# Last context attention of a four-layer network on one core: squares from SBUF, one fixed order for three engines, and the first keys turned beside the layer ahead

## The chip, the cores and the metric

The kernel runs on one core of one Trainium2 chip. The metric is the device time of one execution in microseconds (us), as the median of several runs. A profile of one execution of the kernel before is at hand: its own time, what each engine did and when, and what each instruction waited for. Engines are named as the profile does: PE is TensorE (matmuls), PEld its weight loads, DVE is VectorE, ACT is ScalarE, POOL is GpSimd, SP issues most DMAs.

## The reference, cut to what matters

The network has four layers, each of a cross attention on a context of 2 x 2048 tokens, a mixing block and a feed-forward block, on 2 x 128 tokens of width 256. The change touches the end of the third layer and the cross attention of the fourth, which is this:

```python
def _L3_xattn_ref(draft_hidden, context_hidden, Wq, Wk, Wv, Wo, q_norm_w, k_norm_w, context_position_ids, draft_position_ids):
    B, CTX, DRAFT, D = (2, 512, 64, 256)
    H, KVH, HD = (16, 4, 128)
...
    q = (draft_hidden @ Wq.T).reshape(bsz, draft_len, H, HD)
    q = _rms_norm(q, q_norm_w).transpose(0, 2, 1, 3)
    kv_in = jnp.concatenate([context_hidden, draft_hidden], axis=1)
    k = (kv_in @ Wk.T).reshape(bsz, total_len, KVH, HD)
    v = (kv_in @ Wv.T).reshape(bsz, total_len, KVH, HD).transpose(0, 2, 1, 3)
    k = _rms_norm(k, k_norm_w).transpose(0, 2, 1, 3)
...
    q = _rope(q, draft_position_ids)
    k = _rope(k, full_position_ids)
...
    probs = jax.nn.softmax(scores, axis=-1)
    attn = jnp.einsum('bhqk,bhkd->bhqd', probs, v)
    return attn @ Wo.T
```

Keys and queries are normalised by the root of their mean square (`_rms_norm`), turned by position (`_rope`), and 16 heads of queries share 4 heads of keys and values. With the 128 own tokens, each of the two sequences has 2176 keys, 17 tiles of 128. The block ahead of it is a linear layer with a low-rank update whose two of eight experts are chosen by a gate.

## The kernel before, in words

**Groups.** `l3_xattn` works through eight groups (4 key heads x 2 sequences). For a group, `projected` (line 1448) makes the keys of 8 context tiles in one PSUM tile called `wide` (1024 columns, two of them exist), VectorE copies it to `kq` in SBUF and ScalarE writes its squares to `rot`, reading the same PSUM tile. `own` (1459) does the same for the 128 own tokens: keys, values, and four heads of queries. `summed` (1474) sums the squares on VectorE and takes the root on ScalarE; `rotated` (1479) scales by the inverse root, by the norm's weights, and rotates, all on VectorE, into `rot`. `turn` (1505) transposes 21 tiles of `rot` on TensorE into `kT` and `qT`; VectorE and ScalarE take turns at copying them out of the two PSUM tiles `tr`. `scores` (1521) is called once for each of four heads: four matmuls of 512 keys into two `wide` tiles and one of 128 into `one`; VectorE evicts each with its maximum, makes the scaled maximum `nb`, and ScalarE writes the exponential with its sum. `attend` (1539) transposes the probabilities tile by tile (17 times four), ScalarE copies them to `pT`, and a matmul with `v` adds up in `py`. `out` multiplies by the output weights and adds to `x`.

**What lies beside what.** While group `now` is scored and attended, group `nxt` is projected, normalised and rotated: its first 8 tiles after the first head's scores, its first sums and own tokens after the second head's, its last 8 tiles and the other sums after the fourth head's, its rotations ahead of `attend`. The first group is prepared beside the causal attention of layer three, in smaller steps (line 1583 on).

**What sets the order.** The framework's scheduler puts instructions into each engine's queue by readiness and by program order. The class `InOrder` wraps an engine so that each instruction is queued behind whatever the program put on that engine ahead of it. In `l3_xattn` TensorE and VectorE are wrapped from line 1601 on; ScalarE is not, so there the scheduler chooses.

**The seam.** `l2` and `l3_xattn` are generators; `next(last)` in `l2` runs the next piece of `l3_xattn`. The last call to `linear` (line 1313) is the linear layer for the second sequence. It has three steps: projections, the gate's small operations, and the sum. Beside it `g.busy` (line 137) puts 8 and 12 filler matmuls on TensorE. `l3_xattn` hands it a PSUM bank at line 1602 and goes on with line 1603 only when `linear` has ended: values loaded, 21 tiles turned, then the first scores.

Of the kernel before, what the change touches and what calls it, by code (L numbers as in the profile page):

```python
# [12 lines left out]
F32 = mybir.dt.float32  # L13
# [4 lines left out]
AF = mybir.ActivationFunctionType  # L18
# [4 lines left out]
P = 128  # L23
B = 2
D = 256
# [1093 lines left out]
def l2(g, ctxT, codes, last):  # L1119
# [9 lines left out]
    with tc.tile_pool(name="l2", bufs=1, side="right", reuse_waits="tile") as p:  # L1129
        def mine(name, shape, src):  # L1130
            t = p.tile(list(shape), F32, name=name)
            nc.sync.dma_start(t, src)
            return t

        wkv, wq, wg = (g.load("L2_xattn_" + k) for k in ("Wkv", "Wq", "Wg"))
        bg = mine("bg", [P, 2], g.ins["L2_xattn_bg"])
        wxo = mine("wxo", [P, 2, D], g.ins["L2_xattn_Wo"])
        wqk, wv, wo = (g.load("L2_attn_" + k) for k in ("Wqk", "Wv", "Wo"))
        bqk = mine("bqk", [P, 512], g.ins["L2_attn_bqk"].partition_broadcast(P))
        bv = mine("bv", [P, D], g.ins["L2_attn_bv"].partition_broadcast(P))  # L1140
        bo = mine("bo", [P, D], g.ins["L2_attn_bo"].partition_broadcast(P))
        rot = mine("rot2", [P, 2, 8], g.ins["rope16"])
        cos = rot[:, 0, :].unsqueeze(1).to_broadcast([P, 2 * H, 8])
# [98 lines left out]
        def causal_attention(b):  # L1242
# [5 lines left out]
            g.project(ps, lambda c: xnT[:, c, :], lambda c: wqk[:, c, :])  # L1248
            qk = p.tile([P, 2 * H, 16], F32, tag="qk", name="qk")
            nc.vector.tensor_tensor(qk.rearrange("p h d -> p (h d)"), ps, bqk, ALU.add)  # L1250
            pv = g.mm([P, D])
            g.project(pv, lambda c: xnT[:, c, :], lambda c: wv[:, c, :])
            pad = p.tile([P, 2 * H, 32], F32, tag="pad", name="pad")
            nc.gpsimd.memset(pad, 0.0)
            t1 = p.tile([P, 2 * H, 8], F32, tag="t1", name="t1")
            t2 = p.tile([P, 2 * H, 8], F32, tag="t2", name="t2")
            x1, x2 = qk[:, :, 0:8], qk[:, :, 8:16]
            nc.vector.tensor_tensor(t1, x1, cos, ALU.mult)
            nc.gpsimd.tensor_tensor(t2, x2, sin, ALU.mult)
            t3 = p.tile([P, 2 * H, 8], F32, tag="t3", name="t3")  # L1260
            t4 = p.tile([P, 2 * H, 8], F32, tag="t4", name="t4")
            nc.vector.tensor_tensor(t3, x2, cos, ALU.mult)
# [3 lines left out]

            v = p.tile([P, H, 17], F32, tag="v", name="v")
            nc.gpsimd.memset(v[:, :, 16:17], 1.0)
            nc.vector.tensor_tensor(v[:, :, 0:16], pv.rearrange("p (h d) -> p h d", d=16), bv.rearrange("p (h d) -> p h d", d=16), ALU.add)
            yield  # L1270
            qkT = p.tile([P, 8, P], F32, tag="qkT", name="qkT")
            for j in range(2):
# [7 lines left out]
            for j in range(4):  # L1280

                sc = g.mm([P, 4, P])
                r0 = 32 * j
                for i in range(4):
                    nc.tensor.matmul(sc[:, i, :], lhsT=qkT[r0:r0 + 16, i, :], rhs=qkT[r0:r0 + 16, 4 + i, :], start=True, stop=True)
                S = p.tile([P, 4, P], F32, tag="S", name="S", bufs=4)
                nc.vector.scalar_tensor_tensor(S, sc, -0.25, g.causal.unsqueeze(1).to_broadcast([P, 4, P]), ALU.mult, ALU.subtract)
                nm = g.sm([P, 4], "nm4", bufs=4)
                nc.vector.tensor_reduce(nm, S, AX.X, ALU.min)
                for i in range(4):  # L1290
                    nc.scalar.activation(S[:, i, :], S[:, i, :], AF.Exp, bias=nm[:, i:i + 1], scale=-1.0)
                if b == 0 or j == 0:
                    g.values.step(1)
                tp = g.tr([P, 4, P])
                for i in range(4):
                    nc.tensor.transpose(tp[:, i, :], S[:, i, :], g.ident)
                pT = p.tile([P, 4, P], F32, tag="pT", name="pT", bufs=3)
                nc.vector.tensor_copy(pT, tp)
                for i in range(4):
                    h = 4 * i + j  # L1300
                    nc.tensor.matmul(av[:, h, :], lhsT=pT[:, i, :], rhs=v[:, h, :], start=True, stop=True)
                yield
# [10 lines left out]
        def linear(b, bank):  # L1313
# [5 lines left out]
            pl, pa, po = ps[:, 0:E], ps[:, P:2 * P], ps[:, D:2 * D]  # L1319
            if b == 1:  # L1320
                g.busy(8, ps[:, 0:2 * P])
            g.project(pl, lambda c: xT[:, c, :], lambda c: gw[:, c, :])
# [31 lines left out]
            nc.vector.tensor_tensor(ga, ga, pg, ALU.mult)  # L1354
            if b == 1:
                g.busy(12, po)
            for c in range(2):
# [25 lines left out]
        for _ in causal_attention(1):  # L1383
            next(third, None)
            next(last)
        bank = None
        third = linear(1, lambda: bank())
# [4 lines left out]
        for _ in third:  # L1392
            pass

# [4 lines left out]
def l3_xattn(g, ctxT, cos, sin, values):  # L1399
# [10 lines left out]
    SCALE = float(np.float32(1.0 / np.sqrt(HD)))  # L1410
    pe, dve, pp = nc.tensor, nc.vector, None
    with ExitStack() as ctx:
# [18 lines left out]
        class Group:  # L1431
# [16 lines left out]
            def projected(self, t, n=8):  # L1448
# [7 lines left out]
                dve.tensor_copy(self.kq[:, t:t + n, :], ks)  # L1456
                nc.scalar.activation(self.rot[:, t:t + n, :], ks, AF.Square)

            def own(self):
# [8 lines left out]
                dve.tensor_copy(self.kq[:, NT, :], kv[:, 0:HD])  # L1468
                nc.scalar.activation(self.rot[:, NT, :], kv[:, 0:HD], AF.Square)
                nc.scalar.copy(self.v[:, NT, :], kv[:, HD:2 * HD])  # L1470
                dve.tensor_copy(self.kq[:, KT:NR, :], pq)
                nc.scalar.activation(self.rot[:, KT:NR, :], pq, AF.Square)  # L1472

            def summed(self, lo, hi):
                rs = self.rs[:, lo:hi]
                dve.tensor_reduce(rs, self.rot[:, lo:hi, :], AX.X, ALU.add)
                nc.scalar.activation(rs, rs, AF.Sqrt, bias=g.eps6, scale=1.0 / HD)

# [26 lines left out]
            def turn(self):  # L1505

                self.kT = p2.tile([P, KT * P], F32, tag="kT", name="kT", bufs=1)
                self.qT = p2.tile([P, REP, P], F32, tag="qT", name="qT", bufs=1)
                for k, t in enumerate([KT] + list(range(0, KT, 4))):
                    n = min(4, KT - t) if t < KT else REP  # L1510
# [4 lines left out]
                    if k % 2:  # L1515
                        dve.tensor_copy(out, tp[:, 0:n, :])
                    else:
                        nc.scalar.copy(out, tp[:, 0:n, :])
                    yield

            def scores(self, r):

                S = p2.tile([P, KT, P], F32, tag="S", name="S", bufs=4)
                self.Ss.append(S)
# [11 lines left out]
                dve.tensor_scalar(nm, nm, -SCALE, None, ALU.mult)  # L1536
                nc.scalar.activation(Sf, Sf, AF.Exp, bias=nm, scale=SCALE, accum_out=self.rz[:, r:r + 1])  # L1537

            def attend(self):

                py = pp.tile([P, REP, P], F32, tag="py", name="py", bufs=1)

                def turned(t):
                    tp = g.tr([P, REP, P])
                    for r in range(REP):
                        pe.transpose(tp[:, r, :], self.Ss[r][:, t, :], g.ident)
                    pT = p2.tile([P, REP, P], F32, tag="pT", name="pT", bufs=3)
                    nc.scalar.copy(pT, tp)  # L1548
                    return pT

                pT = turned(0)
                for t in range(KT):
                    nxt = turned(t + 1) if t + 1 < KT else None
                    pe.matmul(py, lhsT=self.v[:, t, :], rhs=pT, start=(t == 0), stop=(t == KT - 1))
                    pT = nxt
                self.yT = p2.tile([P, REP, P], F32, tag="yT", name="yT", bufs=1)
                nc.scalar.copy(self.yT, py)

# [23 lines left out]
        for t in range(0, NT, 2):  # L1582
            now.projected(t, 2)
            values.step()
            if t == 8:
                normed(0)
                now.own()
                now.summed(NT, NR)
            if t == 6:
# [10 lines left out]
        g.ps = pp = ctx.enter_context(tc.tile_pool(name="l3ps", bufs=1, space=PSUM, reuse_waits="tile"))  # L1600
        pe, dve = InOrder(tc, nc.tensor), InOrder(tc, nc.vector)
        yield lambda: pp.tile([P, 512], F32, tag="py", name="py", bufs=1)
        p2 = ctx.enter_context(tc.tile_pool(name="l3s", bufs=2, reuse_waits="tile"))
        now.load()
        for _ in now.turn():
            pass
        normed(1)
        for n in range(len(todo)):
            nxt = Group(*todo[n + 1]) if n + 1 < len(todo) else None
            if nxt:  # L1610
                nxt.load()
            now.Ss = []
            now.rz = g.sm([P, REP], "rz")
            for r in range(REP):
                now.scores(r)
                if nxt and r == 0:
                    nxt.projected(0)
                if nxt and r == 1:
                    nxt.summed(0, 8)
                    nxt.own()  # L1620
                if nxt and r == 3:
                    nxt.projected(8)
                    nxt.summed(8, NR)
            if nxt:
                nxt.rotated(0, 8)
                nxt.rotated(8, NR)
            now.attend()
            turn, out = nxt.turn() if nxt else iter(()), now.out()
# [667 lines left out]
```

## Time and profile before

| | us |
|---|---|
| median of 3 runs (1565.37 to 1567.48) | 1566.69 |
| the profiled execution | 1566.19 |
| its span in the profile | 1564.5 |
| TensorE busy | 1421.2 (91%) |
| VectorE busy | 1136.9 (73%) |
| ScalarE busy | 825.1 (53%) |
| mean granted TensorE clock | 0.913 of full speed |
| first score matmul of the last context attention | at 709.06 |
| start of the eighth group's scores | at 1113.90 |
| last output matmuls of the attention | until 1160.6 |

The page gives busy times over the whole span. A stage is read better from the chain of work that ended last (each step with what released it), from the timeline of a window, and from busy times in stretches, where the granted clock of TensorE stands third from the right as a share of full speed. In lines with a releaser, the idle time just ahead of an instruction is followed by "<-" and the instruction that ended it.

### The profile page before, as it was taken

The numbers are of one execution on the slowest core, as the hardware profiler recorded it, in microseconds if no ns is written. First come the engines' busy times: TensorE is split into PE (matmuls) and PEld (weight loads), VectorE is DVE, ScalarE is ACT, GpSimd is POOL, SyncE is SP. The second block draws the span as 40 slices with busy tenths as digits, with TensorE's granted clock in tenths as the row PEclk, the third lists the DMA queues.
The fourth block names the chain that finished last, engine by engine and source line by source line (L and its number), as shares of the span: only waits on it lengthen the run. The fifth ranks groups of instructions, "written<-read, shape, count | busy, mean of one in ns | idle before, by whom it ended". The sixth has DMA issues, their size and how long they took to land.

```text
span 1564.5 us, 18429 instructions
## 1 busy us (share of the span) xinstructions
PE 1421.2 (91%) x6932; PEld 879.7 (56%) x6932; DVE 1136.9 (73%) x1962; ACT 825.1 (53%) x1260; POOL 148.0 (9%) x140
## 2 busy tenths in 40 slices
PE   8759997898889999978998998998988999999988
PEld 5413333676556777655555555565544566666567
DVE  6889997576456476675775775775726999999976
ACT  3567775323334422435455455455437777777721
POOL 6620002020000000000000000000000111111110
PEclk9955555899999999979999999999989999999999
DMA  6799999644350341410001000000133222221110
GB/s 185 143 178 203 204 202 188 221 149 143 96 182 21 106 135 41 125 54 14 28 5 49 28 17 24 27 28 1 35 121 148 94 95 95 95 94 41 34 34 8
DMA packets 225427, 144.40 MB, mean 92 GB/s; under 512 B 177928, under 2 KB 203801, under 8 KB 220985
## 3 DMA queue, kind: packets, MB, share of 16 engines
q1 hardware_dynamic: 222128, 141.27, 34.5%
q10 hardware_dynamic: 3144, 1.76, 0.4%
q8 instruction: 55, 0.90, 0.2%
q0 software_dynamic: 64, 0.18, 0.1%
q14 instruction: 36, 0.29, 0.1%
HBM read 90.85 MB, written 8.65 MB: 64 GB/s over the span
## 4 chain that ended last, share of the span: by engine, by line
PE 65%; DVE 18%; ACT 9%; DMA 4%; issue 2%; POOL 2%; SPq 0%; DVEq 0%; ACTq 0%; POOLq 0%
PE mm L227 13%; PE mm L184 10%; PE wide L227 9%; PE py L227 7%; DVE S L227 6%; PE pb L227 6%; PE tr L227 5%; DMA pT<-Si 2%; PE acc L1201 2%; PE sc L227 2%; PE acc L227 2%; ACT S L1537 1%; PE one L227 1%; DVE ro L227 1%; POOL kn L227 1%
## 5 line engine op out<-in xcount | busy, mean ns | idle before, releaser
L227 DVE TENSOR_SCALAR_CACHE_REDUCE S<-sc 128x1024 f32<-128x1024 f32 x128 | 150.6, 1219 | 6.8 <-PE sc L227 3.3
L227 PE MATMUL wide<-kT,qT 128*128 128x512 f32 x256 | 128.2, 637 | 25.2 <-ACT rot L1472 20.4
L227 PE MATMUL sc<-kT,qT 48*128 48x512 bf16 x256 | 130.4, 616 | 19.3 <-DMA kT<-kpad 6.5
L227 ACT ACTIVATE Si<-S,nb,sq 128x4096 int16<-128x4096 f32 (+1 forms) x35 | 122.7, 3506 | 43.0 <-issue 27.9
L227 PE MATMUL py<-pT,v 128*128 128x512 f32 x272 | 141.5, 606 | 3.3 <-ACT pT L1548 3.3
L1548 ACT COPY pT<-tr 128x512 f32<-128x512 f32 x136 | 78.2, 584 | 81.0 <-PE tr L227 81.0
L1537 ACT ACTIVATE S<-S,nb 128x2176 f32<-128x2176 f32 x32 | 67.5, 2109 | 93.5 <-DVE nb L227 93.5
L227 DVE TENSOR_SCALAR_CACHE_REDUCE S<-wide 128x1024 f32<-128x1024 f32 x64 | 78.3, 1224 | 51.8 <-PE wide L227 50.6
L227 PE MATMUL pb<-wb,xT 128*128 128x512 f32 x256 | 112.6, 592 | 0.0
L227 PEld LDWEIGHTS tr<-ident,S 128*128 128x128 f32 x544 | 67.8, 142 | 69.7 <-issue 38.8
L227 PEld LDWEIGHTS wide<-kT,qT 128*128 128x128 f32 x256 | 48.5, 203 | 82.7 <-issue 43.5
L227 PEld LDWEIGHTS <-pT 128*128 128x128 bf16 x1024 | 36.5, 105 | 94.8 <-issue 87.8
L227 PE MATMUL tr<-ident,S 128*128 128x128 f32 x544 | 83.1, 275 | 3.7 <-ACT S L1537 3.3
L227 PEld LDWEIGHTS pb<-wb,xT 128*128 128x128 f32 x256 | 48.9, 191 | 60.0 <-issue 55.6
L227 ACT ACT_TABLE_LOAD x53 | 68.0, 1283 | 3.7 <-PE mm L227 3.0
L227 ACT ACTIVATE bc<-pb,rs 128x128 f32<-128x128 f32 x256 | 68.0, 432 | 0.9 <-DVE rs L227 0.9
L227 ACT ACTIVATE bc<-pb 128x1024 f32<-128x1024 f32 x32 | 32.8, 1024 | 64.5 <-PE pb L227 64.5
L227 PE MATMUL mm<-m,xb 128*64 128x128 f32 x512 | 61.7, 279 | 2.9 <-DVE m L227 1.9
L184 PE MATMUL mm<-wvs,ctxT 128*128 128x512 f32 x128 | 61.3, 599 | 0.0
L227 PEld LDWEIGHTS mm<-m,xb 128*64 128x64 f32 x512 | 56.7, 139 | 6.7 <-DVE m L227 2.6
L227 DVE COPY kq<-wide 128x1024 f32<-128x1024 f32 (+2 forms) x28 | 24.0, 855 | 47.7 <-PE wide L227 27.6
L227 PE MATMUL mm<-xT,w 128*128 128x256 f32 x216 | 53.6, 395 | 0.0
(542 smaller groups left out, 2942.7 us busy)
## 6 DMA issues: line engine op xcount, KB each, us to landing
w<-in_L_ffn_w_dram SPq DMA_DIRECT2D x25, 384.0 KB
vs<-st SPq DMA_DIRECT2D x32, 256.0 KB
v<-vs SPq DMA_DIRECT2D x8, 1024.0 KB
wb<-in_L_attn_WB_dram SPq DMA_DIRECT2D x8, 1024.0 KB
wb<-in_L_attn_WC_dram SPq DMA_DIRECT2D x8, 1024.0 KB
bb<-in_L_attn_BC_bias_dram SPq DMA_DIRECT2D x8, 1024.0 KB
ctxT<-in_ctxT_dram SPq DMA_DIRECT2D x15, 512.0 KB
w<-in_ctx_dram SPq DMA_DIRECT2D x8, 512.0 KB
```

Source lines behind the costliest of these rows:

```text
L184: self.nc.tensor.matmul(out, lhsT=lhsT(c), rhs=w(c), start=(c == 0), stop=(c == n - 1))
L227: return lambda *a, **k: self.tc.keep_in_program_order(f(*a, **k))
L1201: nc.tensor.matmul(acc[c], lhsT=kf[:, i, c * P:(c + 1) * P], rhs=cx[:, t % 4 + i, :], start=(t + i == 0), stop=(t + i == NT - 1))
L1537: nc.scalar.activation(Sf, Sf, AF.Exp, bias=nm, scale=SCALE, accum_out=self.rz[:, r:r + 1])
L1548: nc.scalar.copy(pT, tp)
```

## The change

- Squares are made in a function of their own, `squared`, from the keys' copy in SBUF instead of from PSUM, and at other places: the first 8 tiles after the third head's scores, the other 13 inside `attend`. The value copy of `own` goes from ScalarE to VectorE.
- ScalarE is wrapped with `InOrder` too, from the same line as the other two.
- `own` alone follows the second head's scores; the first sums go behind the third's, the first rotation behind the fourth's; the second sums and the second rotation are called inside `attend`, after its fourth tile.
- `turn` goes in another order, with the queries third.
- The first group's turn and its first head's scores are cut into three pieces that `l2` calls between the three steps of `linear`. The filler matmuls are taken out.
- Part of `l2`'s tiles live in a pool that is closed early, and the score tiles lie in two pools.

```diff
@@ l2
-            if b == 1:
-                g.busy(8, ps[:, 0:2 * P])
...
-            if b == 1:
-                g.busy(12, po)
...
         for _ in causal_attention(1):
             next(third, None)
             next(last)
+        early.close()
...
         bank = next(last)
         for _ in third:
-            pass
+            next(last)
@@ l3_xattn
                 dve.tensor_copy(self.kq[:, t:t + n, :], ks)
-                nc.scalar.activation(self.rot[:, t:t + n, :], ks, AF.Square)
+
+            def squared(self, lo, hi):
+
+                act.activation(self.rot[:, lo:hi, :], self.kq[:, lo:hi, :], AF.Square)
...
                 dve.tensor_copy(self.kq[:, NT, :], kv[:, 0:HD])
-                nc.scalar.activation(self.rot[:, NT, :], kv[:, 0:HD], AF.Square)
-                nc.scalar.copy(self.v[:, NT, :], kv[:, HD:2 * HD])
+                dve.tensor_copy(self.v[:, NT, :], kv[:, HD:2 * HD])
                 dve.tensor_copy(self.kq[:, KT:NR, :], pq)
-                nc.scalar.activation(self.rot[:, KT:NR, :], pq, AF.Square)
...
-                for k, t in enumerate([KT] + list(range(0, KT, 4))):
+                for k, t in enumerate([0, 4, KT, 8, 12, 16]):
...
-            def attend(self):
+            def attend(self, beside):
...
+                    if t in beside:
+                        beside[t]()
...
-        pe, dve = InOrder(tc, nc.tensor), InOrder(tc, nc.vector)
+        pe, dve, act = InOrder(tc, nc.tensor), InOrder(tc, nc.vector), InOrder(tc, nc.scalar)
...
         now.load()
-        for _ in now.turn():
-            pass
+        for n, _ in enumerate(now.turn()):
+            if n % 3 == 2:
+                yield
+        now.Ss = []
+        now.rz = g.sm([P, REP], "rz")
+        now.scores(0)
+        yield
...
             for r in range(REP):
-                now.scores(r)
+                if n or r:
+                    now.scores(r)
                 if nxt and r == 0:
                     nxt.projected(0)
                 if nxt and r == 1:
+                    nxt.own()
+                if nxt and r == 2:
+                    nxt.squared(0, 8)
                     nxt.summed(0, 8)
-                    nxt.own()
                 if nxt and r == 3:
                     nxt.projected(8)
-                    nxt.summed(8, NR)
-            if nxt:
-                nxt.rotated(0, 8)
-                nxt.rotated(8, NR)
-            now.attend()
+                    nxt.rotated(0, 8)
+            now.attend({1: lambda: nxt.squared(8, NR), 3: lambda: (nxt.summed(8, NR), nxt.rotated(8, NR))} if nxt else {})
```

## Prediction

> **What bounds the kernel now.** I read the page first: TensorE is busy for 91% of the span, and among its costliest groups the last context attention stands out with a wait that is not a data load.
>
> ```profile
> PE 1421.2 (91%) x6932; PEld 879.7 (56%) x6932; DVE 1136.9 (73%) x1962; ACT 825.1 (53%) x1260; POOL 148.0 (9%) x140
> ...
> L227 PE MATMUL wide<-kT,qT 128*128 128x512 f32 x256 | 128.2, 637 | 25.2 <-ACT rot L1472 20.4
> ```
>
> All 256 score matmuls sit behind 25.2 us of idle, 20.4 of them ended by the square of the queries (line 1472). Next I took the chain that ended last through one steady group, whose first score matmul starts at 823.80. All offsets below count from there.
>
> ```profile
> 832.49 1.03 ACT rot L1457
> 833.52 0.04 issue
> 833.56 2.00 PE wide L227 x4
> ...
> 839.66 1.28 ACT L1477
> 840.95 0.30 ACT rs L1477
> 841.25 0.17 ACT rot L1469
> 841.42 0.16 ACT v L1470
> ...
> 842.33 0.61 ACT rot L1472
> 842.94 0.04 issue
> 842.98 3.53 PE wide L227 x4
> ```
>
> Twice TensorE waits until ScalarE has squared out of PSUM: 0.65 us (the timeline's idle at 833.56) and 2.92 us (at 842.98). After the second, four matmuls take 3.53 us instead of 2.00. That is the clock, as busy time in stretches of 3.41 us shows:
>
> ```profile
> 723.26:726.67 3.41, 2.30 (x6) 0.75 (x4) 0.96 (x2) 3.39 (x5) 0.00 (x0) 1.00 0.48 151
> 726.67:730.09 3.42, 1.63 (x4) 0.87 (x5) 1.83 (x3) 2.26 (x5) 0.00 (x0) 1.00 0.01 2
> ...
> 781.29:784.70 3.41, 0.79 (x2) 0.00 (x0) 1.10 (x2) 2.64 (x7) 0.00 (x0) 1.00 0.00 0
> 784.70:788.11 3.41, 3.13 (x4) 1.51 (x5) 0.73 (x2) 1.51 (x2) 0.00 (x0) 0.50 0.00 0
> ```
>
> The second column is TensorE's busy time, the third value from the right the granted clock. A stretch with 0.79 us busy is followed by one at half clock. In the first group the same wait of 2.90 us lies across two stretches (2.30 and 1.63 busy) and costs no clock. That group takes 56.7 us from score to score (709.06 to 765.77), the next six 58.0 each (chain of waits), the eighth has no successor to prepare.
>
> **The steady group after the change.** All three engines keep the written order from here on, ScalarE newly so. Durations, from the steady group's timeline: scores of one head 3.65 us on TensorE; eight projected key tiles 3.57; own keys and queries 2.58; evicting a 1024-wide score tile 1.23 (the next starts 1.15 later), the 128-wide one 0.29, the scaled maximum done 5.45 after a head's first matmul; exponential 2.11 and 0.19 to read its sum; square of 1024 columns 1.02, so 1.63 for 1664 (estimate, by size); table load 1.28, root 0.30; sums 1.21 and 1.89; rotating the first part 6.74 (858.52 to 865.26), the second 11.16 (to 876.42).
>
> What goes. A square now needs only the copy in SBUF, and the PSUM tile is free when VectorE has copied it: at 8.65 (832.45), while TensorE asks at 8.9. The 0.65 is gone. The own part starts at 10.85 and ends at 13.4; VectorE's three copies (0.28, the value copy moved from ScalarE at the same 0.28, 0.69) end at 14.3. TensorE wants that tile at 15.1. The 2.92 is gone with its half clock. The third head's scores run 13.4 to 17.1, the fourth's 17.1 to 20.7.
>
> What comes instead, first. VectorE's order is: third head's evictions, sum of the first squares, fourth head's evictions. The third maximum is ready at 18.9. ScalarE's order is: third exponential, then the square. So the exponential runs 18.9 to 21.1, the square to 22.15, the sum on VectorE 22.2 to 23.4, and only then comes the fourth head's first eviction, 23.35 to 24.6. Behind the waiting sum stand exactly the evictions that free the two wide tiles, and the second projection needs one of them. TensorE is free at 20.7 and starts at 24.63: a wait of **3.9 us**. It ends at 28.2, when the fourth exponential (26.4 to 28.45, its table loaded before) is just done. So the attend begins at 28.2 at full clock; before it began at 29.99 (853.79).
>
> What comes instead, second. VectorE copies the projected keys 28.4 to 29.6, rotates the first part until 36.25, sums the rest until 38.15. On ScalarE the root for that sum is queued after the fifth transposed tile, and in order: it ends at 38.5, the sixth tile's copy at 39.1. TensorE was ready for it at 36.4: **2.7 us**. The 1.63 square after the third tile costs 0.45 more. The attend of before takes 23.44 (853.79 to 877.23), of which some 0.6 are waits on ScalarE. So it becomes 23.44 - 0.6 + 0.45 + 2.7 = 26.0. The end (turning and output, 877.23 to 881.81 = 4.58) keeps its shape: the order of the pieces changes, not which engine copies how much. Sum: 28.2 + 26.0 + 4.6 = **58.8** at full clock.
>
> The clock. A wait of 3.9 leaves at least 1.95 idle in one stretch of 3.41, and in about seven of ten positions more than 2.7, like the stretch that tripped. One half-clock stretch costs at most 1.7; part lies in the wait itself, and the slowed projections cost 1.5 at 24.6. I take 1.2 a group as a mean over positions, bounds 0 and 3.4 (both waits trip). So **60.0** a group, between 58.8 and 62.2. Seven groups: 420.0 against 56.7 + 6 x 58.03 = 404.9, **+15.1**, bounds +6.7 and +30.5.
>
> By the Trainium skill (TensorE: Matmul & The Clock Gate, "HAM oscillation — how this bites in real kernels") the clock is lost by idle gaps over some 3.4 us; the gaps of before, 2.9, would not be such, and the 3.9 after it would. By that rule alone all of the half clock would be new, seven times up to 1.7, and it speaks against this change; the rows above show that 2.9 is already enough in six groups.
>
> **Bounds of what no row shows.** Squares from SBUF: the exponential, SBUF to SBUF, takes 0.97 ns a column (2.11 / 2176), the PSUM square 1.0; I take equal, 0.3 either way a group (2 us in all). The table load for the late root: at 683.39 one ran before its sum was ready, so it hides in the wait; if it does not, 1.28 x 7 = 9. Loads of values and weights stay on SP's queue in the same order, with a whole group (58 us) of cover; their DMA share in this stage is 0.05 to 0.12. Splitting pools changes only addresses; the following layer's loads wait for the last output matmul (at 1160.6), before and after.
>
> **The start.** In before the linear layer ends on TensorE at 704.4, the turn fills 704.05 to 708.7, scores start at 709.06. Now the turn stands between the linear layer's steps, the first scores behind its last matmul. At most 709.06 - 704.05 = 5.0 goes. The 20 filler matmuls go too: eight delayed the projection from 694.35 (xT copied) to 695.17, 0.8; the twelve ran beside the gate's arithmetic. Against this stand three copies on VectorE (0.69, 0.69, 0.28) and three on ScalarE (0.58 each) between the gate's small steps; at most 3.4 if all of them lie on its path, 0 if all lie in its waits (ScalarE's 1.28 table load is one). And the clock is at half until 702.83 even with the fillers; without them it can return one stretch later, up to 1.7 lost. Together -5.0 - 0.8 + about 1.3 = **-4.5**, bounds -7 and 0. The first phase beside the causal attention stays on TensorE (20.0 of 20 us busy from 660 to 680): squares later there cost nothing; without that cover 0.4 a pair of tiles.
>
> **Sum.** The profiled execution took 1566.19 (span 1564.5), 0.5 below the median 1566.69. 1566.2 + 15.1 - 4.5 = **1577** us.
>
> **Rivals.**
> (1) The clock stays up. Waits move, but none fills a stretch. For it: the first group of before. Against: 3.9 is longer than any wait there. Seven groups of 58.8 give +6.7 - 4.5, so 1568 (1563 to 1571).
> (2) More is lost: both waits trip the clock, or the late root's table load shows as well. For it: 2.7 idle is near the 2.62 of the tripped stretch. At most 30.5 + 9 - 4.5 = 35, so 1601; its middle with the forecast is 1589.
> (3) Faster: the square does not stand behind the third exponential. Its place decides: if ScalarE runs it before 18.9, the sum is made before the fourth head's evictions are due, TensorE waits 0.5 instead of 3.9 there, the late root waits for less (1.8), and a group takes 55.7. Seven: 389.9, -15.0 - 4.5, so 1547. Against it: the third exponential is written first, and the engine's order is fixed in the code. The point is whether the written order is also the one on the engine.
> (4) The start brings nothing: its copies delay the gate by as much as the turn saves. 4.5 more on each case.
>
> **Chances.** Forecast 0.50 (1571 to 1586), (1) 0.20, (2) 0.15, (3) 0.12, the rest 0.03, with (4) spread over the first three. What a measurement of this kernel can tell from no change is about 0.2%, 3.1 us: 1563.6 to 1569.8. (1) gives most of "same" and a little of "faster" by a good start, some of "slower". Faster 0.16, same 0.16, slower 0.68. The range 1562 to 1590 leaves out (3) and the far end of (2).
>
> **What would show it.** Right: no wait of a wide matmul on line 1472's square; instead one of about 3.9 us before the second projection, with VectorE idle before the 8-wide sum until a square has ended; a 2.7 wait of a value matmul behind the late root; half clock after one or both; the first scores at about 705 with no turn before them. Wrong: a square between the second and third exponential, or the fourth head's evictions ahead of the sum; groups below 58 us; or first scores not earlier than 708.

## The result, and the profile after

The changed kernel takes 1586.03 us (median of 4 executions, 1582.81 to 1592.24) against 1566.03 before: the ratio is 1.0125, 95% interval 1.0106 to 1.0145. It is **slower by 20 us**, on the side that was forecast, 9 us above the forecast of 1577 and inside its range. The profiled execution took 1592.24, the longest of the four; its span is 1589.8.

The same two lines of the page, and the two groups of matmuls that now wait most:

```profile
PE 1429.1 (90%) x6912; PEld 896.6 (56%) x6912; DVE 1136.7 (71%) x1970; ACT 821.7 (52%) x1237; POOL 148.2 (9%) x140
...
L227 PE MATMUL py<-pT,v 128*128 128x512 f32 x272 | 142.5, 610 | 19.6 <-ACT pT L227 18.9
...
L227 PE MATMUL wide<-kT,qT 128*128 128x512 f32 x256 | 115.2, 592 | 0.0
...
L227 PE MATMUL wide<-w,ctxT 128*128 128x128 f32 x448 | 71.3, 334 | 25.8 <-DVE S L227 25.8
```

The score matmuls (`wide<-kT,qT`) no longer wait at all: 25.2 us of idle became 0.0. But 25.8 us now stand ahead of the projections (`wide<-w,ctxT`), ended by VectorE's eviction of scores, and 19.6 ahead of the value matmuls, where the page of the kernel before has 3.3:

```profile
L227 PE MATMUL py<-pT,v 128*128 128x512 f32 x272 | 141.5, 606 | 3.3 <-ACT pT L1548 3.3
```

The waits of TensorE within one steady group, first before (823.80 to 881.81), then after (829.46 to 890.84), each with its sum, how many there were, and the longest:

```profile
PE wide L227 <- ACT rot L1472: 2.9, 1, 2.9
PE wide L227 <- ACT rot L1457: 0.7, 1, 0.7
PE py L227 <- ACT pT L1548: 0.5, 2, 0.2
PE one L227 <- DVE x L227: 0.2, 1, 0.2
```

```profile
PE wide L227 <- DVE S L227: 3.7, 1, 3.7
PE py L227 <- ACT pT L227: 2.7, 2, 2.4
PE one L227 <- DVE x L227: 0.2, 1, 0.2
```

The waits have changed places, and grown from 4.3 to 6.6. How the first comes about stands in the timeline of the changed kernel (start, duration, engine, line, operation; in brackets the idle time before it and what ended it):

```profile
848.49 2.11 ACT L227 ACTIVATE S<-S,nb 128x2176 f32<-128x2176 f32 x1 [4.11 <-DVE nb L227]
...
850.60 1.04 ACT L227 ACTIVATE rot<-kq 128x1024 f32<-128x1024 f32 x1
...
851.67 1.22 DVE L227 TENSOR_REDUCE rs<-rot 128x8 f32<-128x1024 f32 x1 [3.21 <-ACT rot L227]
852.80 1.21 DVE L227 TENSOR_SCALAR_CACHE_REDUCE S<-wide 128x1024 f32<-128x1024 f32 x1
...
854.08 6.58 PE L227 MATMUL wide<-w,ctxT 128*128 128x128 f32 x32 [3.68 <-DVE S L227]
```

Read it from the bottom: TensorE waits 3.68 us for an eviction, that eviction stands behind the sum of the squares, the sum waits 3.21 for the square, and the square stands behind the third exponential. And the projections that follow take 6.58 where 3.74 is their time at full clock in the same timeline (the group's first projections, at 833.12). Busy times in the clock's own stretches of the changed kernel (TensorE's busy time second, granted clock third from the right):

```profile
849.63:853.04 3.41, 0.77 (x4) 0.34 (x2) 1.37 (x2) 3.38 (x5) 0.00 (x0) 1.00 0.00 0
853.04:856.45 3.41, 2.37 (x11) 2.37 (x12) 2.65 (x8) 2.15 (x3) 0.00 (x0) 0.50 0.00 0
856.45:859.87 3.42, 3.42 (x18) 3.42 (x18) 0.00 (x0) 1.54 (x2) 0.00 (x0) 0.50 0.00 0
859.87:863.28 3.41, 3.17 (x22) 2.41 (x22) 2.55 (x3) 1.08 (x2) 0.00 (x0) 1.00 0.00 0
```

One stretch with 0.77 busy, and then **two** at half clock, not one: TensorE comes back at 854.08, so the first of them has only 2.37 busy, and only the second, fully busy, brings the clock back.

Where the time went, from score to score: seven groups took 404.8 (709.06 to 1113.90), now 429.1 (707.47 to 1136.54), so +24.2, at 61.4 a group for 58.0 (the first 60.7 for 56.7). From the last causal residual to the first scores it was 19.9 (689.15 to 709.06), now 14.9 (692.60 to 707.47), so -5.0. The last group gives +0.4. Together +19.6; the medians differ by 20.0. The spans of the two profiles differ by 5.7 more, in work that the change does not touch or hardly does: +3.45 ahead of the seam, of which 2.4 stand already at the layer-two residual of line 1113 (531.6 against 534.0), after a stretch of half clock near 465 that the profile of before doesn't have there, and +2.3 after the attention.

### The profile page after: what moved, and what is told of

Same layout as the page of the kernel before. It is cut to its first block, busy times and chain, and to the rows that moved or that the text cites. A ratio compares the mean times of both kernels' runs of the same rounds, so it can differ in the third digit from the quotient of the medians.

```text
span 1589.8 us, 18393 instructions
## 1 busy us (share of the span) xinstructions
PE 1429.1 (90%) x6912; PEld 896.6 (56%) x6912; DVE 1136.7 (71%) x1970; ACT 821.7 (52%) x1237; POOL 148.2 (9%) x140
## 4 chain that ended last, share of the span: by engine, by line
PE 65%; DVE 22%; ACT 6%; DMA 3%; issue 2%; POOL 2%; ACTq 0%; SPq 0%; DVEq 0%; POOLq 0%
PE mm L227 13%; PE wide L227 11%; PE mm L184 10%; DVE S L227 6%; PE py L227 6%; PE pb L227 6%; PE tr L227 4%; PE sc L227 2%; PE acc L1204 2%; DVE kq L227 2%; DMA pT<-Si 2%; PE acc L227 1%; DVE rs L227 1%; PE one L227 1%; DVE ro L227 1%
## 5 line engine op out<-in xcount | busy, mean ns | idle before, releaser
L227 PE MATMUL py<-pT,v 128*128 128x512 f32 x272 | 142.5, 610 | 19.6 <-ACT pT L227 18.9
L227 PE MATMUL wide<-kT,qT 128*128 128x512 f32 x256 | 115.2, 592 | 0.0
L227 PE MATMUL wide<-w,ctxT 128*128 128x128 f32 x448 | 71.3, 334 | 25.8 <-DVE S L227 25.8
L227 PEld LDWEIGHTS wide<-w,ctxT 128*128 128x128 f32 x448 | 69.3, 248 | 27.1 <-DVE S L227 27.1
```

Of the source, the lines that this page charges most:

```text
L227: return lambda *a, **k: self.tc.keep_in_program_order(f(*a, **k))
```

## The experiments

Theory: the two new waits and the half clock of the first cost the time; the seam and the squares from SBUF are gains. Rivals: squares from SBUF, or the fixed order on ScalarE, cost it wherever the sum stands; the seam gives nothing; the half clock has another cause.

| kernel | us | ratio to before, 95% interval | a steady group |
|---|---|---|---|
| changed | 1586.03 | 1.0125 (1.0106 to 1.0145) | 61.4 |
| seam alone | 1564.18 | 0.9977 (0.9960 to 0.9993) | 58.0 |
| squares from SBUF alone | 1526.57 | 0.9730 (0.9705 to 0.9755) | 52.4 |
| changed, first square and sum early | 1542.47 | 0.9850 (0.9816 to 0.9885) | 54.75 |
| changed, filler in the first wait | 1574.35 | 1.0032 (1.0015 to 1.0048) | 58.6 or 60.3 |
| changed, late root | 1565.14 | 0.9997 (0.9974 to 1.0021) | 58.06 |
| changed, both waits taken away | 1529.63 | 0.9772 (0.9730 to 0.9814) | 52.9 |
| seam and squares, order of before | 1524.00 | 0.9729 (0.9696 to 0.9762) | 52.44 |
| changed, ScalarE free | 1546.54 | 0.9853 (0.9810 to 0.9896) | 55.1 or 56.7 |
| changed, first sum behind the evictions | 1555.72 | 0.9918 (0.9887 to 0.9949) | 55.5 or 57.2 |

Ratios are to runs of the kernel before on the same chip; the medians of those runs lie between 1564.43 and 1568.42, so kernels are better compared by their ratios than by their times. Group lengths are from the one profiled execution of each, from one `yT` copy to the next.

**The seam alone.** The kernel before with the first keys turned and scored between the steps of `linear`, the fillers gone, the pools split, the turn in its new order; groups as before.

> The kernel before with one part of the change alone: the first keys turned and the first head scored between the steps of the linear layer, without the filler matmuls. Squares from PSUM and the groups' order as before. My theory: the seam is worth what the two profiles show between the last causal residual and the first scores, 19.9 us before and 14.9 after, so 5.0 us off, about 1561. Rival (the seam gives nothing, its copies delay the gate as much as the turn saves): 1566. Groups stay at 58.0 in both.

It is faster, by 0.23%, about 3.6 us; in its profile the first scores follow the last causal residual after 15.0 us (690.42 to 705.41) instead of 19.9. The steady groups stay at 58.0. The seam gives its 5 us in the profile, and the rival falls. But the first group takes 58.5 where it took 56.7: the wait of 2.9 that cost no clock there in the kernel before (it lay across two stretches) now falls into one, with 0.69 busy (721.40), and half clock follows. So 3.3 of the 5.0 are left, near the 3.6 of the times.

**Squares from SBUF alone.**

```diff
-                nc.scalar.activation(self.rot[:, t:t + n, :], ks, AF.Square)
+                nc.scalar.activation(self.rot[:, t:t + n, :], self.kq[:, t:t + n, :], AF.Square)
...
-                nc.scalar.activation(self.rot[:, NT, :], kv[:, 0:HD], AF.Square)
-                nc.scalar.copy(self.v[:, NT, :], kv[:, HD:2 * HD])
+                dve.tensor_copy(self.v[:, NT, :], kv[:, HD:2 * HD])
                 dve.tensor_copy(self.kq[:, KT:NR, :], pq)
-                nc.scalar.activation(self.rot[:, KT:NR, :], pq, AF.Square)
+                nc.scalar.activation(self.rot[:, NT:NR, :], self.kq[:, NT:NR, :], AF.Square)
```

> The kernel before with another part alone: squares read from the copy in SBUF, the value copy on VectorE; order, seam and fillers as before, ScalarE ordered by the scheduler. My theory: the two waits of 0.65 and 2.92 us and the half clock after them (1.5) go, and nothing takes their place, because the first sum is still made after the second head's scores, from a square that is long done. Six groups of 58.0 become about 53, the first 56.7 becomes 53: some 34 us off, 1532. Rival (squares from SBUF are what made the changed kernel slow): 1575 or more. Rival (another wait of the old order takes over): 1550 to 1566.

1526.57 us: this part by itself is worth 2.7%. In its steady groups (820 to 1060) TensorE waits for nothing but these:

```profile
PE py L227 <- ACT pT L1547: 2.3, 10, 0.2
PE one L227 <- DVE x L227: 0.9, 4, 0.2
```

That is 3.2 us in four to five groups, and none of the seven has half clock. All of the old wait, and its half clock, came from the PSUM tile being held until ScalarE, the second reader, had come to it in its own queue; no new wait takes its place in the old order. (What the moved value copy does by itself is not tested apart from the squares.)

**First square and sum early.** The changed kernel with these lines:

```diff
                 if nxt and r == 0:
                     nxt.projected(0)
+                    nxt.squared(0, 8)
                 if nxt and r == 1:
                     nxt.own()
-                if nxt and r == 2:
-                    nxt.squared(0, 8)
                     nxt.summed(0, 8)
```

> The changed kernel with the first square directly behind the first projection and the first sum behind the own part, everything else as changed. My theory: the wait of 3.7 us ahead of the second projection and the two half-clock stretches behind it (3.0) go; the late root still holds ScalarE for about 2 us in the attend. 61.4 becomes 54.5 to 56 a group: 1540 to 1548. Rival (one fixed order on ScalarE, or squares from SBUF, cost the time wherever the sum stands): 1580 or more.

1542.47, groups of 54.75: the first wait and its two half-clock stretches are gone, 6.7 a group, with squares from SBUF and one fixed order on all three engines still in place. The wait behind the late root is left (2.1 the longest).

**Filler in the first wait.** The changed kernel with 32 matmuls of 256 columns, read by nobody, ahead of `nxt.projected(8)`.

```diff
                 if nxt and r == 3:
+                    ps = pp.tile([P, 512], F32, tag="py", name="py", bufs=1)
+                    for _ in range(32):
+                        pe.matmul(ps[:, 0:2 * P], lhsT=g.identb, rhs=g.ident.bitcast(BF16), start=True, stop=True)
                     nxt.projected(8)
```

> The changed kernel with 32 filler matmuls of 256 columns, whose result nothing reads, on TensorE ahead of each second projection, where it waits 3.7 us. They change no data dependency: the wait on VectorE's eviction stays. My theory: the wait costs what it did but the clock stays up, the projections take 3.6 instead of 6.6: 3.0 off a group, 21 in all, about 1565. Rival (the half clock comes from elsewhere in the group, or the time is bound by the wait alone): 1586, and more if the fillers themselves delay the projection.

1574.35: 12 of the 21 us (14.6 by the ratios). Its timeline in one group:

```profile
849.70 3.66 PE L227 MATMUL py<-ident,identb 128*128 128x256 bf16 x32
853.54 3.84 PE L227 MATMUL wide<-w,ctxT 128*128 128x128 f32 x32 [0.19 <-DVE S L227]
```

The fillers occupy the wait, and the projections are back at 3.84 as printed (6.58 without them). So the half clock is a cost of its own, and this wait is its cause. Four of the six groups take 58.64, which is the group at full clock with both waits in it, 2.8 less than 61.4; two take 60.3, with one stretch of half clock left. That one comes from the other wait: the value matmul at 807.72 waits 2.41 behind the late root, and 2.04 of that lie in one stretch (805.68 to 809.09, 1.37 busy), after which half clock follows. In the changed kernel the same wait lies across two stretches (2.21 and 2.19 busy from 866.69) and costs no clock. The median therefore gains less than seven times 2.8.

**Late root.** Only the call moves, from the fourth to the seventh tile of the attend.

```diff
-            now.attend({1: lambda: nxt.squared(8, NR), 3: lambda: (nxt.summed(8, NR), nxt.rotated(8, NR))} if nxt else {})
+            now.attend({1: lambda: nxt.squared(8, NR), 6: lambda: (nxt.summed(8, NR), nxt.rotated(8, NR))} if nxt else {})
```

> The changed kernel with the second sum, its root and the second rotation called after the seventh tile of the attend instead of the fourth. My theory: the root no longer holds ScalarE's queue while VectorE is still rotating, so the 2.4 us wait in the attend goes; the first wait and its half clock stay. By the waits alone 61.4 becomes 59 to 59.5 a group, 1570. Rival (the group is locked to the clock's stretches of 3.413 us: 61.44 is 18 of them, and a shorter group waits longer or runs longer at half clock until the next multiple): groups stay at 61.4 or fall to 58.0, so 1585 or 1562.

Here my theory by waits alone was too small: 1565.14, and groups of 58.06, not 59. The first wait is still 3.68; the waits of the value matmuls fell from 2.7 to 0.5 a group. The rest is the clock, one stretch at half instead of two:

```profile
845.23:848.64 3.41, 0.93 (x8) 0.93 (x9) 3.35 (x4) 2.90 (x4) 0.00 (x0) 1.00 0.00 0
848.64:852.06 3.42, 3.42 (x19) 3.42 (x18) 0.68 (x6) 2.20 (x2) 0.00 (x0) 0.50 0.00 0
852.06:855.47 3.41, 3.17 (x23) 2.41 (x23) 2.22 (x3) 1.08 (x2) 0.00 (x0) 1.00 0.00 0
```

TensorE is back at 847.71, before the half-clock stretch begins; that stretch is fully busy and is the last, and the projections take 5.47 instead of 6.58. So of the 3.3 that a group gained, 2.2 are the waits and 1.1 the clock. The rival that named 58.0 had the length nearly right, but its reason, a group locked to 17 stretches, is not shown: the two terms add up without it, and the groups stay at 58.06 where 17 stretches are 58.02.

**Both waits taken away.** The edits of the two runs together.

> The changed kernel with both: first square and sum early, second sum and root late. My theory: neither wait is left, no half clock in the groups: 54.75 a group (the run with the early sum alone) less some 2 us, 52.5 to 53; seven groups 13 us less than that run, about 1526. Rival (late root work pushes the second rotation past the end of the attend, and the turn waits for it): 1535 or more, with a wait of the turn on the rotation.

1529.63, groups of 52.9, no half clock in any of the seven. Of the changed kernel's 61.4, 8.5 were the two waits and what the clock made of them.

**Seam and squares in the order of before.** The seam's edit and the squares' edit together, ScalarE ordered by the scheduler.

> The seam and the squares from SBUF together, in the order of before, ScalarE ordered by the scheduler. My theory: the two are independent, so 1526.6 less the seam's 4: 1522. Rival (the seam costs back what the squares gave, or the groups fall to a half clock again): 1526 to 1540.

1524.00, ratio 0.9729: **it beats both kernels**, the one before by 2.7%. Its groups are those of the squares alone (52.44), and so is its ratio (0.9730 there), so the seam's share here is not shown by the times. In the two profiles the first `yT` copy comes 6.2 earlier (747.51 against 753.68). The split pools and the new order of the turn are in this run too, so it is not they that cost the changed kernel its time.

**ScalarE free.** The changed kernel with `InOrder` on TensorE and VectorE only.

> The changed kernel with ScalarE ordered by the scheduler again in the groups; TensorE and VectorE keep the written order. My theory: the wait comes from the place of the first sum in VectorE's order; the square can at best move ahead of the third exponential, and if the scheduler leaves it behind, nothing changes: 1580 to 1590. Rival (the fixed order on ScalarE is the cause): a square ahead of the third exponential and 1545 or less.

1546.54 (the profiled execution was the slowest of four, 1554.56): **here my theory as I put it fell.** I had blamed the place of the sum in VectorE's order. That place is unchanged here, and the wait is 0.4. The rival's sign, a square ahead of the third exponential, is there; its 1545 or less was missed by 1.5. The scheduler puts the square right behind the copy, ahead of the second exponential, in ScalarE's queue:

```profile
886.41 1.06 ACT L1460 ACTIVATE rot<-kq 128x1024 f32<-128x1024 f32 x1 [0.99 <-DVE kq L227]
...
890.45 2.11 ACT L1538 ACTIVATE S<-S,nb 128x2176 f32<-128x2176 f32 x1 [2.98 <-DVE nb L227]
...
896.63 1.21 DVE L227 TENSOR_REDUCE rs<-rot 128x8 f32<-128x1024 f32 x1
896.75 2.11 ACT L1538 ACTIVATE S<-S,nb 128x2176 f32<-128x2176 f32 x1 [4.10 <-DVE nb L227]
...
899.04 3.84 PE L227 MATMUL wide<-w,ctxT 128*128 128x128 f32 x32 [0.37 <-DVE S L227]
```

The second and third exponential stand at 890.45 and 896.75, the square ahead of both, so the sum starts at 896.63 without waiting. The new theory: the wait needs two things at once, a square fixed behind the third exponential and a sum fixed ahead of the fourth head's evictions. Early square and sum had taken away both; this run takes away the first alone. The last run takes away the second alone.

**First sum behind the evictions.** Changed kernel, the square where it is.

```diff
                 if nxt and r == 2:
                     nxt.squared(0, 8)
-                    nxt.summed(0, 8)
                 if nxt and r == 3:
+                    nxt.summed(0, 8)
                     nxt.projected(8)
```

> The changed kernel with only the first sum and its root moved, behind the fourth head's evictions; the square stays behind the third exponential in ScalarE's fixed order. Theory, as the run with a free ScalarE left it: the wait needs both, a square behind the third exponential and a sum ahead of the evictions; taking away either ends it. Then the 3.7 us wait and its half clock go here too; the root with two table loads (2.9 us) now stands between the fourth exponential and the first transposed tile and costs 1 to 2 us there, and the late root's wait stays: 55.5 to 57 a group, 1545 to 1557. Rival (the place of the square alone decides): a wait of 3 us or more ahead of the second projection stays and the time is 1575 or more.

1555.72, within what was expected. No wait of a projection is left among TensorE's waits from 820 to 1060:

```profile
PE py L227 <- ACT pT L227: 12.8, 8, 1.9
PE one L227 <- DVE x L227: 1.1, 5, 0.2
```

The root with its table loads now shows at the start of the attend (a wait of 1.32 at 852.98), and groups alternate between 55.5 and 57.2 with a half-clock stretch in every other one, where the late root's wait of 1.88 lies within one stretch (802.42 to 805.84, 1.54 busy). So the wait ahead of the second projection needs both conditions; with either alone it is gone.

## Why the prediction was right, and where its size was off

- **What goes.** Right: the waits on the squares of lines 1457 and 1472 are gone. The squares from SBUF take 1.04 for 1024 columns and 1.59 for 1664, against 1.02 and 1.63 put in. The run with this part alone shows what it is worth: 2.7%.
- **First new wait, 3.9.** Right: 3.68, before the second projection, with VectorE idle 3.21 ahead of the sum.
- **Second new wait, 2.7.** Right: 2.43, behind the late root; its table load lies hidden in the wait, as taken.
- **The group at full clock, 58.8.** Right: 58.64 in four of six groups of the filler run.
- **The clock, 1.2 a group as a mean over positions.** This is the term that was mis-sized: it measured 2.8 (61.4 less 58.64). The prediction counted one half-clock stretch, partly hidden in the wait. The projections lost 2.8 (6.58 for 3.74), because two stretches ran at half: the wait reaches 1.04 us into the first of them, and that stretch, 70% busy (2.37 of 3.41), did not bring the clock back. Nor was there a mean over positions. The prediction's "about seven of ten positions" is under six of ten when worked out, but that hardly matters: in the last run half clock followed a stretch with 1.54 busy, 1.87 idle, and the prediction itself had 1.95 idle as the least that a wait of 3.9 leaves in one stretch. So half clock was due wherever such a wait fell, and six of the seven groups settled on nearly one place of the grid. So 61.4 a group for 60.0, +24.2 in seven for +15.1. With 24.2 in place of 15.1 the sum would have been 1586.
- **The start, -4.5.** Right: -5.0 between the profiles, and 0.9977 (0.9960 to 0.9993) alone.
- **The range.** 1586 is the upper end of the band given to the forecast (1571 to 1586), and nearer to rival 2's middle (1589) than to 1577. The direction and the waits were understood; that the total lies inside owes something to a range that reached to 1590.
- **Rival 1** (no half clock, 1568) fell: half clock follows the first wait in all seven groups, for one stretch in the first and two in the others. **Rival 3** (1547) named one of the two deciding places: the square before or behind the third exponential. In the changed kernel it is behind, so the forecast held; with ScalarE free it is ahead, and the time is 1546.5. That the two times agree so well is luck in part: 55.7 a group comes out only with the clock's 1.2 still in it (58.8 - 3.4 - 0.9 + 1.2), which the rival doesn't say. And the last run shows that a square behind the exponential does no harm ahead of the projections if the sum stands behind the evictions. **Rival 2** was right that more is lost, but not by its mechanism: in the changed kernel the second wait costs no stretch of its own and the root's load does not show. That the second wait can cost a stretch at half clock, where most of it lies in one stretch, the filler run and the last run show. **Rival 4** fell.
- **The rule of the Trainium skill** (TensorE: Matmul & The Clock Gate, "HAM oscillation — how this bites in real kernels") warns of gaps over some 3.4 us. The gap of 3.68 brings half clock, as it says; but the one of 2.92 did so in the kernel before as well, and so did those of 2.41 in the filler run and of 1.88 in the last run, each wholly or for the most part inside one stretch. So the measurement decides against that bound.

## What to carry to other kernels

Before an order is fixed on an engine, go through each instruction that waits for another engine and ask what stands behind it in its own queue: a small sum waiting for a square held up the evictions that fed TensorE, and freeing either the square or the sum was enough. Test the parts of a change one by one: here two parts were gains of 2.7% and 0.2%, and the third, the order of the calls with ScalarE fixed in it, turned the whole into a loss of 1.3%. Price a wait of TensorE together with the clock, by the busy share of the stretches that it touches.

## What the runs showed of the hardware

- The clock's stretches lie on a fixed grid of 3.413 us: in the clock record of the traces the clock changes only after whole multiples of it. A steady group of the kernel before has 54.61 at full clock and 3.41 at half, which is 17 stretches or 58.02; one of the changed kernel has 54.61 and 6.83, 18 stretches or 61.44.
- The groups of these kernels settle on such a length (from score to score): 61.32, 61.38, 61.41, 61.42, 61.44 and 61.43 in the changed kernel. In the run of the seam alone a group of 58.34 is followed by 57.88, 57.96, 57.98 and 58.02, so the delay is made good. With the late root, where the half-clock stretch is fully busy, it is not: a group of 58.35 is followed by 58.06, as before it. What draws a group to the grid no run tests by itself.
- In the groups, a stretch with up to 1.54 us busy of 3.41 was followed by half clock (0.66 to 1.07 in the changed kernel, 1.37 in the filler run, 1.54 in the last run, 802.42). Those with 1.60 (before, 726.65) and 1.64 (last run, 1085.73) were not. At the seam one with 1.95 was (ScalarE free, 703.40), so busy time may not be the whole of it.
- At half clock, a stretch with 2.37 busy of 3.41 did not bring full clock back (changed, 853.04); nor did those of 2.78 and 2.87 at the seam of the kernel before (692.60 to 699.42). Stretches of 3.13 (before, 784.70), 3.07 (before, 699.42) and 3.42 (late root, 848.64) did. But so did one of 2.87 (seam alone, 898.89), and one of 3.23 did not (squares alone, 690.77). So no bound of busy time fits all of them, and what decides is not settled.
